# Weaving the first four scan steps of a channel tile between the last four of the tile before

## The chip, the cores and the metric

The kernel runs on one core of a Trainium2 chip, in one launch, all in fp32. The metric is the device time of that core in microseconds (us). Three runs of the kernel before took 17002.24, 17006.93 and 17012.62 us; the median, 17006.93 us, is the time before.

## What is computed

Two layers follow each other on a batch of eight images of 192 channels and 64 x 64 pixels. The change concerns the first, whose core is a gated scan in four directions over 384 channels:

```python
def gate_scan(X, L, Gl, Gm, Gr, chunk):        # chunk = 8: 8 steps, 8 chunks side by side
    h0 = zeros(B, C, H, W // chunk)
    def step(h, inp):
        x, l, gl, gm, gr = inp
        hn = l * x + gl * shift_up(h) + gm * h + gr * shift_down(h)
        return hn, hn
...
x = dwconv3x3(conv1x1(x, W_in)) + b_dw
p = conv1x1(x, W_xd)                           # 16 channels
xs = the 4 directions of x: rows, columns, and both reversed
Gl, Gm, Gr = the three parts of conv1x1(p, W_w), each divided by |Gl| + |Gm| + |Gr| + 1e-7
out = gate_scan(xs, conv1x1(p, W_l), Gl, Gm, Gr, 8) * conv1x1(p, W_u) + xs * conv1x1(p, W_d)
y = sum over d of w_m[d] * out[d]
y = conv1x1(grn(layernorm(y)), W_out)
```

The first of the eight steps of a scan starts from a state of zero. So it is only `l * x`: the gates Gl, Gm and Gr, their norm and the neighbours drop out of it. The second layer, two Mamba blocks on the 64 x 64 tokens of each image, is not touched.

## The kernel before, in words

The first layer is tile_ss2d_kernel. It goes through the images one by one. While the projections and the depthwise convolution of image b run, the normalisation and the output projection of image b-1 are woven in; then `scan` (line 347) runs alone.

A scan has 96 steps: 3 channel tiles c of 128 channels, 8 steps j, 4 directions d, in this order of nesting. A step works on 128 partitions x 512 elements (8 chunks x 64). The state of direction d is one tile of `states` (line 104), with a column of zeros on either side, and is used again by the next channel tile.

What a step does is cut into short methods of the class Step, one or a few instructions each. The order of the work is written out by hand: the kernel is built in manual_schedule, so that each engine gets its instructions in the order in which the Python code issues them. The loop at line 361 lays four steps over each other: s0 computes its neighbour products and norm, s1 its sum, s2 its state and output products, s3 its output sums, and `ahead` starts its gates. The parts that matter here, by engine:

- TensorE: `gates` and `up` (line 237) multiply 16 projected channels with the gate weights. A step has six gates, a step with j=0 only three (l, then d and u). `total` (line 273) adds the neighbour products by two matmuls with the identity. `add` (line 329) adds the two output products of the four directions in PSUM, again with the identity; for d=2 (JOINED) the second one is left out, and GpSimd has joined it to that of d=3 (line 315).
- VectorE: `neighbour` (L263, three products), `norm` (L278, two additions), `newton` (L294, L295), `mix` (L299) and `output` (L319). A j=0 step has only the last.
- ScalarE: absolute values (L247, L250), logarithm and exponential for the reciprocal (L283, L288), the copies of two gates from PSUM to SBUF, `decay` (L254, lam) and `direct` (L310, dx), and `store` (L339), which copies the sum of four directions out.
- GpSimd: `entry` (L257, l times x), `pair` (L267), `state` (L303) and `bypass` (L313, and L315 for d=3).

[...]gl, gm, q and yp one each, gr and c two each. The gates l, d and u of every step take turns in the two buffers of "c"; a buffer is free again when its gate has been copied by ScalarE (l, d) or multiplied by VectorE (u). In SBUF "dx" and "hu" have two buffers each. The pools reuse whichever buffer has become free, and the instruction that writes into it waits for the last one that used it.

## Time and profile before

| | us |
|---|---|
| median of three runs | 17006.93 |
| the profiled execution | 16998.62 |
| its span, first to last instruction | 16996.8 |
| first layer (until the last output copy at 5974.1) | about 5990 |
| TensorE busy, whole span | 15880.5 (93%) |
| VectorE busy | 15268.1 (90%) |
| GpSimd busy | 15164.6 (89%) |
| ScalarE busy | 11938.6 (70%) |

In the profile PE is TensorE, DVE VectorE, ACT ScalarE and POOL GpSimd. A line of a timeline gives the start of an instruction or of a run of equal ones in us from the start of the span, its duration, engine, line, operation, output and inputs, and in brackets how long the engine had been idle before it and what ended that. An fp32 matmul has two records here, so x4 after a line stands for two matmuls. A line of the table of stages gives the stretch, its length, the busy time and number of instructions of PE, PE's weight loads, DVE, ACT and POOL, then the clock that TensorE was granted (1.00 is full), the share of the DMA engines and GB/s.

The eight scans take some 520 to 530 us each from their first store to their last. Their boundaries between channel tiles, two in each scan, are 16 in all. In the middle of a tile all four compute engines run almost without pause: in the stretch from 264 to 287 us PE is busy for 23.0 of 23 us, DVE for 22.6, POOL for 22.4 and ACT for 15.4. In the stretch from 304 to 327 us, at a boundary, it is 22.3, 13.3, 20.8 and 9.3.

### The profile page before, as it was taken

The page shows a single profiled execution, that of the slowest core. Times are in us where ns is not written, and L with a number is a line of the kernel's source. Part 1 is how long each engine was busy: PE and PEld are TensorE (multiplying, and loading weights), DVE is VectorE, ACT ScalarE, POOL GpSimd, SP SyncE. Part 2 cuts the span into 40 slices and gives each one's busy share as a digit, 9 for nine tenths or more (in the row PEclk, how much of TensorE's full clock was granted, in tenths as well). Part 3 has the DMA queues.
Part 4 walks back from the last instruction along what each step waited for, and adds up shares of the span by engine and source line. Part 5 has one row for each costly group of instructions (what it writes and reads, how often), then busy time and mean ns, then how long its engine had stood idle before and what let it go on. Part 6 is the DMA issues. An engine that isn't in the chain of part 4 may idle for free.

```text
span 16996.8 us, 151143 instructions
## 1 busy us (share of the span) xinstructions
PE 15880.5 (93%) x42192; PEld 6479.2 (38%) x42192; DVE 15268.1 (90%) x14474; ACT 11938.6 (70%) x25451; POOL 15164.6 (89%) x9955
## 2 busy tenths in 40 slices
PE   9999999999999989999999999999999999999998
PEld 2333333333333334444444444444444444444443
DVE  8888888888887779999999999999999999999999
ACT  5656666666666667777777777777777777777777
POOL 7787978778787779999999999999999999999999
PEclk8999999999999999999999999999999999999999
DMA  1001010010100022222222222222222222222222
GB/s 30 24 7 30 1 30 9 22 30 1 30 1 26 3 95 105 105 105 105 104 106 104 106 104 106 104 106 104 106 104 106 104 106 104 106 104 103 106 102 87
DMA packets 695389, 1247.33 MB, mean 73 GB/s; under 512 B 311768, under 2 KB 378672, under 8 KB 694544
## 3 DMA queue, kind: packets, MB, share of 16 engines
q1 hardware_dynamic: 694144, 1237.37, 19.9%
q8 instruction: 335, 5.49, 0.1%
q14 instruction: 510, 4.18, 0.1%
q10 hardware_dynamic: 400, 0.29, 0.0%
HBM read 1178.77 MB, written 58.72 MB: 73 GB/s over the span
## 4 chain that ended last, share of the span: by engine, by line
DVE 26%; ACT 9%; POOL 9%; issue 8%; DMA 8%; PE 5%; SPq 0%; DVEq 0%; POOLq 0%; ACTq 0%
DVE da L848 18%; DMA c_sb<-bc 7%; POOL hs L834 6%; ACT da L840 3%; DVE hs L855 3%; DVE hs L848 3%; PE yp L860 2%; PE dbl_ps L721 1%; POOL hs L855 1%; DVE z L786 1%; DMA b_sb<-bc 1%; ACT xc L713 1%; ACT L713 1%; POOL e L756 1%; ACT xt L650 1%
## 5 line engine op out<-in xcount | busy, mean ns | idle before, releaser
L834 POOL TENSOR_TENSOR hs<-dtx,b_sb 128x1022 f32<-128x1022 f32 x3072 | 7140.1, 2351 | 62.1 <-DMA b_sb<-bc 29.8
L848 DVE TENSOR_TENSOR_SCAN da<-da,hs 128x1024 f32<-128x1024 f32 x2560 | 5852.5, 2286 | 497.0 <-ACT hs L843 462.8
L860 PE MATMUL yp<-hs,ident 128*128 128x512 f32 x12288 | 5764.5, 603 | 47.9 <-POOL hs L855 25.4
L840 ACT ACTIVATE da<-dt,a 128x512 f32<-128x512 f32 x6144 | 4246.7, 691 | 435.9 <-DVE hs L848 257.5
L860 PEld LDWEIGHTS yp<-hs,ident 128*128 128x128 f32 x12288 | 2316.7, 193 | 3058.9 <-issue 2700.9
L855 DVE TENSOR_TENSOR hs<-da,c_sb 128x1024 f32<-128x1024 f32 x2560 | 3129.3, 1222 | 88.4
L237 PE MATMUL g<-xp,w_gate_sb 16*128 16x512 f32 x8640 | 1816.2, 658 | 60.4 <-ACT dx L310 51.6
L851 ACT COPY state<-da 128x2 f32<-128x2 f32 x2560 | 399.4, 156 | 1981.8 <-DVE hs L855 1972.8
L700 PE MATMUL pc<-xr,conv_diag 128*128 128x512 f32 x3072 | 1572.3, 642 | 170.4 <-ACT dt L746 151.9
L678 PE MATMUL pi<-xT,in_w 96*128 96x512 f32 x3072 | 1447.2, 597 | 79.3 <-ACT y L816 36.5
L263 DVE TENSOR_TENSOR q<-g,h 128x512 f32<-128x512 f32 x2016 | 1351.4, 684 | 115.5 <-PE g L237 70.0
L273 PE MATMUL q<-q,ident 128*128 128x512 f32 x2688 | 1333.5, 619 | 0.0
L283 ACT ACTIVATE rc<-g,eps 128x512 f32<-128x512 f32 x672 | 462.0, 687 | 1116.7 <-DVE g L278 1116.7
L313 POOL TENSOR_TENSOR dx<-dx,xc 128x512 f32<-128x512 f32 x768 | 1079.5, 1406 | 156.6 <-ACT dx L310 133.6
L848 DVE TENSOR_TENSOR_SCAN hs<-da,hs 128x1024 f32<-128x1024 f32 x512 | 1167.5, 2280 | 57.2 <-POOL hs L834 57.2
L855 POOL TENSOR_TENSOR hs<-hs,c_sb 128x1024 f32<-128x1024 f32 x512 | 1204.9, 2353 | 1.2 <-ACT state L851 1.2
L267 POOL TENSOR_TENSOR q<-q,q 128x512 f32<-128x512 f32 x672 | 852.7, 1269 | 196.5 <-DVE q L263 190.9
L237 PEld LDWEIGHTS g<-xp,w_gate_sb 16*128 16x128 f32 x8640 | 495.0, 188 | 1304.9 <-DVE q L263 394.3
L700 PEld LDWEIGHTS pc<-xr,conv_diag 128*128 128x128 f32 x3072 | 584.8, 198 | 1029.0 <-issue 660.8
L257 POOL TENSOR_TENSOR lam<-lam,xc 128x512 f32<-128x512 f32 x672 | 942.0, 1402 | 33.3 <-ACT lam L254 33.3
L278 DVE TENSOR_TENSOR g<-g,ab 128x512 f32<-128x512 f32 x1344 | 933.0, 694 | 22.8
L196 DVE SCALAR_TENSOR_TENSOR xc<-pi,dw_sb,xc 128x504 f32<-128x504 f32 (+3 forms) x1152 | 839.5, 736 | 98.4 <-POOL xc L162 63.8
(140 smaller groups left out, 22975.2 us busy)
## 6 DMA issues: line engine op xcount, KB each, us to landing
b_sb<-bc SPq DMA_DIRECT2D x1024, 512.0 KB, 9.0
c_sb<-bc SPq DMA_DIRECT2D x1024, 512.0 KB, 8.9
xin<-in_x_dram SPq DMA_DIRECT2D x192, 384.0 KB, 3.6
mid<-ot SPq DMA_DIRECT2D x128, 192.0 KB, 2.1
xt<-mid SPq DMA_DIRECT2D x64, 384.0 KB, 10.0
out_dram<-y SPq DMA_DIRECT2D x64, 384.0 KB, 2.6
bc<-dbl SPq DMA_DIRECT2D x128, 64.0 KB, 1.6
b<-bc SPq DMA_DIRECT2D x128, 8.0 KB, 7.3
```

The costliest lines, as they stand in the source:

```text
L237: nc.tensor.matmul(dst, self.wg[r, at, self.d, :], flat(self.xp[r, self.j]), start=True, stop=True)
L257: nc.gpsimd.tensor_mul(self.lam if self.j else self.hc, self.lam, direction(self.xc, self.d, self.j))
L263: nc.vector.tensor_mul(self.q[i], rows(self.g[i]), self.h[:, :, i : i + HW])
L273: nc.tensor.matmul(self.sum, ident, flat(term), start=(i == 0), stop=(i == 1))
L313: nc.gpsimd.tensor_mul(self.dx, self.dx, direction(self.xc, self.d, self.j))
L678: nc.tensor.matmul(pi, self.m.in_w[:, i, c * P : (c + 1) * P], self.tokens.xT[:, i, :], start=(i == 0), stop=(i == 1))
L700: nc.tensor.matmul(pc, self.m.conv_w[:, c, t, :], self.xr[c][:, t : t + T], start=(t == 0), stop=(t == 3))
L834: nc.gpsimd.tensor_mul(self.hs[:, :, 1:], dtx, self.p.b_sb[self.g][:, :, 1:])
L840: nc.scalar.activation(self.da[:, n, :], self.p.dt[self.c], AF.Exp, scale=self.p.m.a[:, self.c, at : at + 1])
L848: nc.vector.tensor_tensor_scan(h, da, hs, 0.0, ALU.mult, ALU.add)
L855: engine.tensor_mul(self.hs, self.h, self.p.c_sb[self.g])
L860: nc.tensor.matmul(self.p.yp[self.c], ident, self.hs[:, n, :], start=False, stop=stop)
```

## The change

The steps of a scan are put in another order. At each of the two boundaries the four j=0 steps of the next channel tile, which stood behind the four j=7 steps of the tile that ends, are set between them: j=7 d=0, j=0 d=0, j=7 d=1, j=0 d=1 and so on. The loop that overlaps steps is as before. Since two channel tiles are now under way at once, there are eight states, four for even and four for odd tiles. The output sum of a tile needs the one bank "yp" until its last step, so the woven steps don't use it: their products are added by VectorE, straight into the output tile y in SBUF (seven additions for the four directions), and neither the store nor the joining of d=2 and d=3 is done for them. The j=0 steps of the first channel tile stay as they were.

```diff
-    for d in range(ND):
+    for d in range(2 * ND):
         states.append(const.tile([P, CHUNK, HW + 2], F32, name=f"h{d}"))
         nc.gpsimd.memset(states[d], 0.0)
...
-            self.h = states[d]
+            self.h = states[c % 2 * ND + d]
+
+            self.beside = c > 0 and j == 0
...
-            if self.d == JOINED + 1:
+            if self.d == JOINED + 1 and not self.beside:
                 nc.gpsimd.tensor_add(self.dx, self.dx, self.before.dx)
...
+            term = (self.hu, self.dx)[i]
+            if self.beside:
+                if self.d or i:
+                    nc.vector.tensor_add(self.y, flat(term if self.d else self.hu), self.y if self.d else flat(term))
+                return
...
-            if self.d == ND - 1:
+            if self.d == ND - 1 and not self.beside:
                 nc.scalar.copy(self.y, self.yp)
...
-        ys, steps = [], [Nothing()] * 4
+        ys = [big.tile([P, CHUNK, CHUNK * HW], F32, tag="big", name=f"y_{b}_{c}") for c in range(NC)]
+        done = []
         for c in range(NC):
...
+            tile = []
             for j in range(CHUNK):
...
+                for d in range(ND):
+                    tile.append(Step(f"{b}_{c}_{j}_{d}", xc[c], xp, ys[c][:, j, :], c, d, j))
+                    tile[-1].before = tile[-2] if d else None
+
+            for last, step in zip(done[-ND:], tile[:ND]):
+                done.insert(done.index(last) + 1, step)
+            done += tile[ND if c else 0 :]
+        steps = [Nothing()] * 4 + done
```

More of the change, by code (lines that the diff above doesn't have):

```diff
@@ L218, with __init__ @@
     class Step:
-        def __init__(self, tag, xc, xp, wg, d, j):
-            self.tag, self.xc, self.xp, self.wg, self.d, self.j = tag, xc, xp, wg, d, j
+        def __init__(self, tag, xc, xp, y, c, d, j):
+            self.tag, self.xc, self.xp, self.y, self.d, self.j = tag, xc, xp, y, d, j
+            self.wg = w_gate_sb[:, :, :, c * P : (c + 1) * P]
             self.q, self.ab = {}, {}
-            self.h = states[d]
+            self.h = states[c % 2 * ND + d]
+            self.beside = c > 0 and j == 0
             self.hc = self.h[:, :, 1 : HW + 1]
@@ L331, in add @@
                     ident,
-                    flat((self.hu, self.dx)[i]),
+                    flat(term),
                     start=(self.d == 0 and i == 0),
@@ L347, in scan @@
     def scan(b, xc, xp):
-        ys, steps = [], [Nothing()] * 4
+        ys = [big.tile([P, CHUNK, CHUNK * HW], F32, tag="big", name=f"y_{b}_{c}") for c in range(NC)]
+        done = []
         for c in range(NC):
-            wg = w_gate_sb[:, :, :, c * P : (c + 1) * P]
-            ys.append(big.tile([P, CHUNK, CHUNK * HW], F32, tag="big", name=f"y_{b}_{c}"))
+            tile = []
             for j in range(CHUNK):
-                steps += [Step(f"{b}_{c}_{j}_{d}", xc[c], xp, wg, d, j) for d in range(ND)]
-                for step in steps[-ND:]:
-                    step.y = ys[c][:, j, :]
-        for before, step in zip(steps[4:], steps[5:]):
-            step.before = before
+                for d in range(ND):
[5 more added lines that the diff above has]
+        steps = [Nothing()] * 4 + done
         steps += [Nothing()] * 4
```

## The prediction

> **What bounds the kernel now.** The page's busy table comes first, to rank the engines:

> ```profile
> PE 15880.5 (93%) x42192; PEld 6479.2 (38%) x42192; DVE 15268.1 (90%) x14474; ACT 11938.6 (70%) x25451; POOL 15164.6 (89%) x9955
> ```

> Three engines lie within four points, so the stage decides. Second, TensorE's timeline inside a channel tile. One step's cycle:

> ```profile
> 269.94 1.98 PE L273 MATMUL q<-q,ident 128*128 128x512 f32 x4
> 271.86 1.14 PE L237 MATMUL g<-xp,w_gate_sb 16*128 16x512 f32 x8
> 272.93 1.13 PE L329 MATMUL yp<-hu,ident 128*128 128x512 f32 x2
> 273.89 1.02 PE L329 MATMUL yp<-dx,ident 128*128 128x512 f32 x2
> 274.84 1.13 PE L237 MATMUL g<-xp,w_gate_sb 16*128 16x512 f32 x4
> ```

> Start to start: neighbour sum 1.92 us, four gates 1.07 (or a lone one, 1.05), two output sums 0.96 each, two gates 1.06. No line has an idle bracket: TensorE is the bound. A step is 5.95 us, 5.10 where d=2 leaves out one output sum, so four take 22.97 us. Third, ScalarE's timeline at a tile's end, which clocks the groups of four by their store:

> ```profile
> 309.64 0.61 ACT L339 COPY y<-yp 128x512 f32<-128x512 f32 x1
> ...
> 334.08 0.58 ACT L339 COPY y<-yp 128x512 f32<-128x512 f32 x1 [2.96 <-PE yp L329]
> ...
> 358.72 0.60 ACT L339 COPY y<-yp 128x512 f32<-128x512 f32 x1
> ...
> 381.75 0.60 ACT L339 COPY y<-yp 128x512 f32<-128x512 f32 x1
> ```

> From the store of j=6 to that of the next tile's j=1 pass 72.1 us here; over the 16 tile boundaries 67.5 to 73.4, mean 71.8. One plain group off, 48.8 us remain for j=7 and the next j=0 together, 25.8 more than j=7 alone. Why do four steps with a third of the work cost that? TensorE's timeline in the gentlest boundary, then the stages' clock in the first:

> ```profile
> 1982.08 1.12 PE L237 MATMUL g<-xp,w_gate_sb 16*128 16x512 f32 x2 [0.67 <-ACT dx L310]
> 1983.13 1.13 PE L329 MATMUL yp<-hu,ident 128*128 128x512 f32 x2
> 1984.19 1.13 PE L237 MATMUL g<-xp,w_gate_sb 16*128 16x512 f32 x4
> 1986.06 2.07 PE L237 MATMUL g<-xp,w_gate_sb 16*128 16x512 f32 x2 [0.75 <-ACT dx L310]
> ```

> ```profile
> 315.00:320.00 5.00, 5.00 (x13) 1.75 (x12) 2.29 (x4) 1.17 (x2) 4.64 (x5) 1.00 0.00 0
> ...
> 325.00:330.00 5.00, 4.26 (x7) 1.00 (x6) 0.69 (x1) 0.58 (x1) 3.16 (x3) 0.50 0.00 0
> ```

> The brackets show a chain: with two PSUM buffers for "c", the next gate waits until ScalarE has copied the bypass gate (0.7 us). A j=0 step is 1.05 + 0.96 or 1.92 + 1.06 + 0.7 us. And the same gate then takes 2.07 instead of 1.12: the clock (third column from the end) is halved. Asked in slices of 0.2 us, the clock in the first boundary is at half for 10.2, 3.4 and 3.5 us, 17 in all; in the gentlest, where the excess is 21.5 us, once for 6.8.

> [...]before both drops TensorE idles only 0.7 us of 3.4. Weighting the matmuls by the rows they feed (an identity sum 128 of 128, a gate 16) sorts this trace: the windows from 1982.4 (0.41) and 320.0 fall, those from 1979.0 (0.48) and 1996.1 (0.45) hold[...]. That weighting is my reading. [...]

> **The change, part by part.** F0..F3 are the j=7 steps, Z0..Z3 the next tile's j=0 steps, now ordered F0 Z0 F1 Z1 F2 Z2 F3 Z3. The built program's order confirms it; the steps issue no DMA, so SP's queue is as before.

> *Removed at each boundary:* 7 output sums (TensorE, 7 x 0.96 = 6.7 us), one store (ScalarE, 0.6), one joining add (GpSimd, 1.23). *Added:* 7 VectorE additions, 7 x 0.60 = 4.2 us. Four memsets of 0.54 us at the start lie beside the first loads: nothing; uncovered, 2.2 us. *Moved:* per Z step two ScalarE copies, three gates, two GpSimd products (2.73 us the pair), one VectorE product.

> Loads per F+Z pair: TensorE 5.74 + 2.11 = 7.85; GpSimd 5.49 + 2.73 = 8.22; VectorE 5.66 + 0.60 + 1.05 = 7.31. By load alone four pairs need 33 us against 48.8, and the gain would be 16 x 16 = 250 us. I don't believe it, because the pair has a longer chain. Around TensorE's queue: neighbour sum of F 1.92, four gates of the next F 1.07, two output sums of the earlier F 1.92, its two gates 1.06; copy of its bypass gate 0.7 (ScalarE); lone gate of Z 1.05; copy of that 0.7, because the third use of "c" needs its bank; last gate of the earlier Z 1.05; only then the next neighbour sum, queued behind. Sum 9.5 us. What hid the copies before, the neighbour and output sums, Z no longer has: its output sums are the part that moved. VectorE stays inside: from the gates' start 4.9 us to the end of the two norm additions (as between 335.83, the gates, and 339.31 + 1.42), one addition, hu at 6.1, in time for the Z gates at 6.5.

> ```profile
> 337.11 0.69 DVE L263 TENSOR_TENSOR q<-g,h 128x512 f32<-128x512 f32 x1 [1.19 <-PE g L237]
> 338.10 1.29 DVE L263 TENSOR_TENSOR q<-g,h 128x512 f32<-128x512 f32 x2 [0.30 <-ACT ab L250]
> 339.31 1.42 DVE L278 TENSOR_TENSOR g<-g,ab 128x512 f32<-128x512 f32 x2
> ```

> Laid out at full clock from F0's first product: F0's neighbour sum ends at 7.6, as in the steady rows. F1's ends at 17.6 (10.0: this pair still carries output sums of an earlier full step), F2's at 27.2, F3's at 36.7. Then a new wait. "dx" has two buffers; F2's is held until F3 joins it, so F3's copy waits for the one of Z2, which VectorE frees with its addition. Behind F3's copy stand, on ScalarE, the logarithm of the next step and, on TensorE, the next four gates, which need the copied bank. Layout: gates 36.7, VectorE's products and norm to 41.5, addition, hu, addition to 43.4, copy 44.1, gates to 45.3, copy, gate to 47.0, neighbour sum to 48.9. In steady running that sum ends at 7.6: four pairs cost 41.4 us.

> *Half clock.* The present boundaries: the gentlest has 21.5 excess with 6.8 us at half clock, of which 6.1 worked, so 3.1 lost and 18.4 left; the mean 25.8 loses 7.4. After: between the output sums' end and the next neighbour sum lie 4.5 us per pair with gates alone, weight under 0.2[...]. Walking four phases through the chain: the clock falls once per such pair and the sum's end moves by 1.7, 3.1, 3.8 and 1.7, mean 2.6. This holds for F2 and F3: 5.2. For F1, with output sums between, two phases in three and 2.3: 1.5. The wait after F3 (8.3 us from 38.7 to 47.0) surely drops it: gates 1.07, gate 1.05, sum 1.92 doubled, 4.1. Sum 10.8.

> [...]Unseen, so bounded: nothing if an addition only pushes GpSimd back (it has 1.3 us of room per 9.5); a whole product of 1.2 to 1.5 us ahead of hu for F3 and the step after, and again ahead of F3's copy: 4. [...]I take 1.5.

> Together 41.4 + 10.8 + 1.5 = 53.7 against 48.8: 4.9 us longer, times 16 = 78 us. The profiled execution took 16,998.6 (span 16,996.8), 8 below the median 17,006.9; 17,077 in its terms, 17,085 for the median. The second layer and the stages between scans are untouched.

> **Rivals.** *The clock holds* (other side): if Z's gates beside denser steps keep TensorE at full speed, 41.4 + 1.5 = 42.9, 5.9 less, 94 us: 16,913. It decides wherever less than 5.9 us per boundary is lost to half clock. For it: fewer bare j=0 steps in a row, and a threshold I inferred. Against: 4.5 us of gates alone. *The clock costs what it does now:* 41.4 + 7.4 + 1.5 = 50.3, 24 us more: 17,031. [...]4 us plus as much lost clock behind it, 57 or more: 17,150 to 17,200. That the change doesn't do what it says is excluded by the order.

> **Numbers.** The measurement tells about 0.2% (34 us) from no change. Forecast, slower, 0.45; clock holds, faster, 0.25; clock as now, same, 0.18; port, slower, 0.12. So faster 0.25, same 0.18, slower 0.57. Range 16,915 to 17,195; the slower cases alone 17,041 to 17,195.

> **What would show it.** Right: stores of j=6 to j=1 near 77 us; no output sums between the gates of Z and the next neighbour sum, brackets of 0.7 there; F3's copy idle on a VectorE addition; half-clock spells in the F2 and F3 pairs. Wrong: clock 1.00 through the boundary; the pair near 8.2 with GpSimd full (the chain misread); additions far above 0.7 us or GpSimd products stretched (port).

## The result, and the profile after

| | before | after |
|---|---|---|
| median of 5 runs, us | 17006.93 | 17079.14 |
| lowest to highest, us | 17002.24 to 17012.62 | 17070.02 to 17084.80 |
| ratio after/before, 95% interval | | 1.0043, 1.0032 to 1.0055 |
| span of the profiled execution, us | 16996.8 | 17067.9 |
| mean granted TensorE clock | 0.962 | 0.956 |

The change makes the kernel slower by 72 us, 0.4%. The forecast was 17,085.

The busy table of the page after:

```profile
PE 15913.8 (93%) x41968; PEld 6479.9 (38%) x41968; DVE 15377.4 (90%) x14586; ACT 11942.2 (70%) x25435; POOL 15168.9 (89%) x9943
```

TensorE has 224 records fewer (112 output sums) and is yet busy for 33 us more; VectorE has its 112 additions. A TensorE that does less work in more time is the first sign of its clock, whose mean fell from 0.962 to 0.956.

Next, ScalarE's timeline at the first tile boundary, the stores that clock the groups of four:

```profile
306.74 0.59 ACT L347 COPY y<-yp 128x512 f32<-128x512 f32 x1 [0.36 <-PE yp L337]
354.09 0.59 ACT L347 COPY y<-yp 128x512 f32<-128x512 f32 x1 [1.50 <-PE yp L337]
384.18 0.60 ACT L347 COPY y<-yp 128x512 f32<-128x512 f32 x1
```

They are the stores of j=6, j=7 and the next tile's j=1; the one between is gone. They lie 77.4 us apart here, 75.2 to 81.6 over the 16 boundaries, mean 78.5. In the changed kernel the store of j=6 itself comes earlier, so this pair holds a little of what was before it. A wider stretch is fairer, from the store of j=5 to that of the next tile's j=3. Its mean went from 140.7 to 146.1 us, 5.4 per boundary, 87 in all. The other parts of a scan, measured between the same stores, are the same to 0.1 us in both (114.9 before the first stretch, 45.9 between the two, 83.2 behind the second). The remaining -16 of the span's difference lie outside these stretches, -10 of it behind the last scan, for the most part in the second layer, which wasn't changed.

TensorE's timeline in that boundary (idle brackets as before):

```profile
299.69 1.14 PE L240 MATMUL g<-xp,w_gate_sb 16*128 16x512 f32 x8
300.76 1.13 PE L337 MATMUL yp<-hu,ident 128*128 128x512 f32 x2
301.81 1.13 PE L240 MATMUL g<-xp,w_gate_sb 16*128 16x512 f32 x4
303.67 1.12 PE L240 MATMUL g<-xp,w_gate_sb 16*128 16x512 f32 x2 [0.72 <-ACT dx L313]
...
312.59 1.13 PE L240 MATMUL g<-xp,w_gate_sb 16*128 16x512 f32 x4
314.44 3.92 PE L240 MATMUL g<-xp,w_gate_sb 16*128 16x512 f32 x6 [0.72 <-ACT dx L313]
318.29 3.78 PE L276 MATMUL q<-q,ident 128*128 128x512 f32 x4
322.01 1.64 PE L240 MATMUL g<-xp,w_gate_sb 16*128 16x512 f32 x8
...
335.94 1.13 PE L240 MATMUL g<-xp,w_gate_sb 16*128 16x512 f32 x4
340.01 4.73 PE L240 MATMUL g<-xp,w_gate_sb 16*128 16x512 f32 x12 [2.95 <-DVE hu L322]
344.67 3.78 PE L276 MATMUL q<-q,ident 128*128 128x512 f32 x4
...
358.53 1.40 PE L240 MATMUL g<-xp,w_gate_sb 16*128 16x512 f32 x4 [0.43 <-DVE hu L322]
```

The reader is to see three things. The brackets of 0.72 before the lone gates of Z1 and Z2 (303.67, 314.44) are the chain through "c". At 318.29 a neighbour sum (two matmuls) takes 3.78 us instead of 1.98: the granted clock is 0.50 there. And ahead of 340.01 TensorE stands for 2.95 us. The bracket names VectorE's hu, which freed one of the two buffers of "c". But ScalarE's timeline shows what was late, since its copy would have freed the other one some 2 us earlier. This is an estimate: F3's gates end at 337.07, and a gate behind such a copy waits 0.7 us.

```profile
340.67 0.59 ACT L313 COPY dx<-g 128x512 f32<-128x512 f32 x1 [3.58 <-DVE y L330]
341.15 0.69 ACT L286 ACTIVATE rc<-g,eps 128x512 f32<-128x512 f32 x1
```

This is F3's copy, waiting for its buffer until VectorE has added Z2's product (L330), with the logarithm behind it. The same 3.58 us stand there in all 16 boundaries.

Last, the table of stages at 3.4 us a row (the clock is the third column from the end):

```profile
333.40:336.80 3.40, 3.40 (x16) 0.91 (x14) 2.04 (x4) 1.78 (x4) 2.05 (x2) 1.00 0.00 0
336.80:340.20 3.40, 0.45 (x6) 0.19 (x8) 3.37 (x7) 0.29 (x1) 1.96 (x2) 0.99 0.00 0
340.20:343.60 3.40, 3.40 (x11) 1.37 (x12) 1.50 (x3) 2.74 (x6) 2.19 (x2) 0.50 0.00 0
343.60:347.00 3.40, 3.40 (x6) 1.18 (x4) 3.33 (x6) 1.53 (x4) 2.65 (x3) 0.50 0.00 0
```

In the second row TensorE works 0.45 us of 3.4, while VectorE is full (3.37) with products, norm, addition, hu and addition; the row after runs at half clock, and that lasts to 353.8. In slices of 1 us the stretch contains 30.1 us at half clock per boundary, against 16.6 before.

### One account for all kernels

For each kernel the stretch splits into three parts: TensorE's waits (those of gates and neighbour sums on hu, dx, lam and rc in the first layer, divided by 16), what is lost to half clock (an estimate: half of the time at half clock, since a neighbour sum then took 3.78 us instead of 1.98 and a lone gate 2.07 instead of 1.12), and the rest, TensorE's work at full speed. All in us per boundary; the ratio is to the kernel before on the same chip.

| kernel | ratio (95%) | stretch | waits | lost to half clock | rest |
|---|---|---|---|---|---|
| before | 1 | 140.7 | 3.2 | 8.3 | 129.2 |
| after | 1.0043 (1.0032 to 1.0055) | 146.1 | 6.5 | 15.0 | 124.6 |
| e1 own dx buffer | 1.0012 (1.0006 to 1.0019) | 142.7 | 5.6 | 13.0 | 124.1 |
| e2 after, fillers | 0.9992 (0.9985 to 0.9999) | 139.3 | 2.2 | 2.5 | 134.6 |
| e3 e1 and fillers | 0.9974 (0.9964 to 0.9983) | 138.7 | 2.0 | 4.5 | 132.2 |
| e4 e1, one addition | 1.0015 (1.0008 to 1.0021) | 143.4 | 3.5 | 14.5 | 125.4 |
| e5 before, fillers | 0.9966 (0.9953 to 0.9978) | 136.1 | 0.4 | 1.9 | 133.8 |
| e6 after, old order | 1.0012 (1.0006 to 1.0019) | 141.9 | 5.5 | 13.9 | 122.5 |
| e7 after, later sums | 1.0093 (1.0078 to 1.0109) | 149.6 | 1.8 | 20.7 | 127.1 |
| e8 before, thin fillers | 0.9986 (0.9980 to 0.9993) | 139.8 | 0.4 | 7.3 | 132.1 |
| e9 e7 and fillers | 1.0021 (1.0012 to 1.0029) | 142.5 | 1.6 | 4.6 | 136.3 |
| e10 e6 and fillers | 1.0004 (0.9996 to 1.0012) | 141.2 | 2.3 | 6.1 | 132.8 |
| e11 before, wide gates | 0.9925 (0.9912 to 0.9939) | 133.8 | 3.2 | 1.8 | 128.8 |
| e12 e1 and wide gates | 0.9980 (0.9972 to 0.9988) | 140.1 | 5.8 | 10.5 | 123.8 |

After against before: 4.6 us less work for TensorE, 3.3 more of waiting, 6.7 more lost to half clock, 5.4 in sum. That the rest is much the same (124.6, 124.1, 125.4, 123.8) in the four woven kernels without fillers or later sums supports the account. In every kernel 0.4 of the waits lies at the ends of the scans and not in the stretch; it drops out of the differences.

### The profile page after: what moved, and what is told of

The parts are those of the page before. It is cut to its first block, busy times and chain, and to the rows that moved or that the text cites. A ratio compares the mean times of both kernels' runs of the same rounds, so it can differ in the third digit from the quotient of the medians.

```text
span 17067.9 us, 150795 instructions
## 1 busy us (share of the span) xinstructions
PE 15913.8 (93%) x41968; PEld 6479.9 (38%) x41968; DVE 15377.4 (90%) x14586; ACT 11942.2 (70%) x25435; POOL 15168.9 (89%) x9943
## 4 chain that ended last, share of the span: by engine, by line
DVE 27%; ACT 9%; POOL 9%; issue 8%; DMA 7%; PE 4%; SPq 0%; DVEq 0%; POOLq 0%; ACTq 0%
DVE da L859 19%; DMA c_sb<-bc 6%; POOL hs L845 6%; DVE hs L866 4%; ACT da L851 3%; DVE hs L859 3%; POOL hs L866 1%; PE dbl_ps L732 1%; PE yp L871 1%; DVE z L797 1%; DMA b_sb<-bc 1%; ACT xc L724 1%; ACT L724 1%; POOL e L767 1%; POOL lg L769 1%
## 5 line engine op out<-in xcount | busy, mean ns | idle before, releaser
L240 PE MATMUL g<-xp,w_gate_sb 16*128 16x512 f32 x8640 | 1895.3, 676 | 107.2 <-DVE hu L322 52.9
L276 PE MATMUL q<-q,ident 128*128 128x512 f32 x2688 | 1443.2, 662 | 5.7 <-DVE rc L302 5.7
L306 POOL TENSOR_TENSOR h<-lam,rc 128x512 f32<-128x512 f32 x672 | 856.8, 1275 | 167.4 <-DVE rc L302 166.7
L260 POOL TENSOR_TENSOR lam<-lam,xc 128x512 f32<-128x512 f32 x672 | 940.7, 1400 | 30.1 <-ACT lam L257 29.6
```

The source lines that it names most:

```text
L240: nc.tensor.matmul(dst, self.wg[r, at, self.d, :], flat(self.xp[r, self.j]), start=True, stop=True)
L260: nc.gpsimd.tensor_mul(self.lam if self.j else self.hc, self.lam, direction(self.xc, self.d, self.j))
L276: nc.tensor.matmul(self.sum, ident, flat(term), start=(i == 0), stop=(i == 1))
```

## The experiments

The theory behind the prediction: the woven order gives TensorE spells of gates alone, so its clock is halved for longer, and the buffer of dx adds a wait. Rivals: VectorE's additions are what costs, by their own time or by what they and GpSimd's products lose to each other (in the changed kernel a product of 1.27 us took 2.01 and an addition of 0.68 took 1.28); or the longer chain costs by itself, and the clock only follows. The kernel before, run again beside each series of experiments, took 16,999.67 to 17,006.93 us as the median, so a difference of some 7 us between runs of different series says nothing.

### e1: a dx buffer of its own for d=2

```diff
-            self.dx = self.work("dx")
+            self.dx = self.work("dj", 1) if self.d == JOINED and not self.beside else self.work("dx")
```

> The changed kernel, with a buffer of its own for the bypass product of d=2 (of every step that is not woven), so that the copy for d=3 no longer waits until VectorE has added that of the woven step. My theory: TensorE's idle stretch of 3 us before the gates after the last pair goes, and with it part of the half-clock spell of 13.6 us that follows: 4 to 6 us per boundary, 16,985 to 17,015 us. Rival, the additions themselves[...] make the change slow and the buffer is a detail: under 1 us per boundary, 17,060 to 17,080.

Measured: 17,022.82, 56 below the change, 22 above before. Both theories had the sign, and the time is 8 above the upper end of the theory's. No copy into dx waits for an addition any more. This is worth 3.4 us per boundary (146.1 to 142.7), of which 0.9 is TensorE's waiting and 2.0 half clock, but it is not all that the change costs.

### e2: identity matmuls in the weave

```diff
+            fill(0 if not (getattr(s1, "beside", False) is True) else 4 if s1.d == ND - 1 else 1)
             ahead.gates()
...
+            fill(1 if getattr(s1, "beside", False) is True else 0)
```

`fill(n)` issues n matmuls of the identity with 128x512 of xc into the bank q; nobody reads the result. It stands ahead of and behind the gates of the iterations whose s1 is woven, four times ahead of the last.

> The changed kernel with useless identity matmuls into the free bank q, where TensorE waits between the output sums and the next neighbour sum: one before and one after the woven step's gate, four before the gates that wait longest. Nothing reads them. My theory (weight per window sets the clock): the clock stays at full speed through the boundary; some 27 us at half clock per boundary, about 10 of them lost, are saved, at a cost of 0.3 us per filler that is longer than the wait it sits in: 8 us per boundary less, about 16,950 us, faster than before too. Rival (the clock falls for another reason, or the chain of copies, not the clock, makes the boundary long): the half-clock spells stay and ten added matmuls of 0.96 us cost 2 to 9 us per boundary, 17,110 to 17,220 us.

Measured: 16,986.54, 93 below the change, although TensorE has 11 more matmuls of 0.96 us per boundary. The theory said 16,950: the sign is right, the size too hopeful. Half clock fell from 30.1 to 4.9 us per boundary. TensorE's timeline now shows a pair of 10.2 us with hardly a gap, so the fillers' own time eats part of the gain. The buffer's wait is still there (ScalarE idle for 3.58 us ahead of 339.20), now beside four fillers on TensorE.

### e3: both

Edit of e1, and one filler on either side of the gates.

> Both: the buffer of its own for d=2 and one filler before and one after the gates wherever the step ahead of the neighbour sum is a woven one. My theory: the layout at full clock without the buffer wait, 38 to 40 us in place of 48.8 before and 53.7 after: 16,840 to 16,880 us. Rival[...]: no better than the better of the two alone, 16,950 or more.

Measured: 16,954.12. That is 74 above the theory's range. It lies at the edge of the rival's range of time, but the rival is wrong too in what it said, since this is 32 better than the better of the two alone. The two edits of 56 and 93 give 125 together. What stays: TensorE itself is full in the pairs (10.2 us), and behind the weave lies a wait that no edit touched:

```profile
352.71 1.89 PE L240 MATMUL g<-xp,w_gate_sb 16*128 16x512 f32 x4 [1.16 <-DVE hu L322]
354.64 3.78 PE L276 MATMUL q<-q,ident 128*128 128x512 f32 x4
```

It is the iteration in which Z3 would add its outputs on TensorE. It has nothing to add, TensorE runs ahead of VectorE, and the clock falls once more.

### e4: e1 without six of the seven additions

```diff
-                if self.d or i:
+                if self.d == 0 and i:
```

It leaves out the outputs of d=1, 2 and 3 at j=0 of the second and third tile.

> As the kernel with the buffer of its own for d=2, but of the seven additions of a boundary only the first is left: the outputs of directions 1 to 3 are left out at j=0 of the second and third channel tile. [...]My theory: 1 to 2 us per boundary, 15 to 35 us less than the kernel with the additions. Rival[...]: 4 to 8 us per boundary, 65 us or more less.

Measured: 17,023.25, the same as e1. The additions, with what they and GpSimd's products lose to each other, cost nothing that shows in the time, and neither expectation held (15 to 35 below e1, or 65 and more). But TensorE waits less without them (3.5 for 5.6 us), and the half clock takes most of that back (14.5 for 13.0). What the additions would cost at full clock isn't shown.

### e5: the filler in the kernel before

```diff
+            fill(1 if bare(s1) else 0)
             ahead.gates()
```

`bare` is true for the j=0 steps of the second and third tile.

> The kernel before, with one identity matmul of 128x512 into a bank of the pool q (its result is not read) ahead of the gates in each iteration whose s1 is a step of j=0 of the second or third channel tile: it stands where the missing neighbour sum would stand. If the half clock is what a boundary loses, before as after, then before has it too: some 16.6 us at half clock per boundary, at about 0.45 us each 7.4 us, less some 1 to 1.5 us that the four matmuls (0.94 us each) cost where nothing hides them. Theory: half clock in the stretch below 6 us per boundary, time 16,890 to 16,930, and the change made on top of fillers (the earlier run with fillers, 16,986) is then slower than this by 50 or more. Rival, the clock is only a sign and the waits for VectorE and GpSimd set the boundary: 17,000 to 17,030, with the half clock gone or not.

Measured: 16,940.41, at 3.8 us of half clock. The theory held, with a time 10 us above its range and e2 46 us slower than this where 50 or more was expected. The rival, that the clock is only a sign, is out: it had 17,000 to 17,030. The boundaries of this one kernel also price the half clock: 13 of 16 have none and take 134.3 us, the three others have 20.5 and take 144.1. So 9.8 us are lost to 20.5 at half clock.

With fillers in both, the woven order gains nothing: 16,954 (e3, with the buffer mended) against 16,940, two ratios whose intervals overlap. The feeding isn't equal, though: e3 carries eight fillers per boundary where e5 has four, and it still has 9.0 us at half clock.

### e6: the old order, with the additions kept

```diff
-            for last, step in zip(done[-ND:], tile[:ND]):
-                done.insert(done.index(last) + 1, step)
-            done += tile[ND if c else 0 :]
+            done += tile
```

> The changed kernel with its order undone: the four steps of j=0 follow the last four of the tile before, as in the kernel before; eight states and VectorE's additions of the outputs stay. So TensorE has neither neighbour sum nor output sum in four iterations that follow each other, while the chain (gates, copies, product, state) stays the one of the kernel before. Theory, the time is set by the chain and by the clock, and TensorE is fed least here: four iterations without sums are some 4 x 1.92 us less work for TensorE, which the chain doesn't let through, the half clock as long as before or longer (16 to 25 us per boundary): 17,000 to 17,080. Rival 1, the weaving itself is what makes the change slower and the additions are harmless or a gain: below 17,000. Rival 2, VectorE's additions are what costs: as slow as the changed kernel, 17,080 or more.

Measured: 17,022.51, within the theory's range. So moving the output sums to VectorE costs 18 us by itself, with no weave. It takes TensorE's work at the boundary from 129.2 to 122.5 us and gives 5.6 back to half clock and 2.3 to waits. The weave without its buffer wait (e1) has the same ratio; the wait is the other 56.

### e7: the sums spread over the woven iterations

Three buffers for dx, the two output sums of an F step one iteration later, on either side of the woven step's lone gate, and Z's lam copied ahead of the logarithm.

```diff
-            self.dx = self.work("dx")
+            self.dx = self.work("dx", 3)
...
+            if behind and woven:
+                s4.add(0)
             ahead.gates()
...
+            if behind:
+                s4.add(1)
```

> The changed kernel with three edits at the boundary: three buffers for dx (and for the squares that share them); the output sums of the last four steps of a tile are issued one iteration later, so that each iteration of the weave, the woven step's too, has work for TensorE of nearly the same amount; and the woven step's lam is copied ahead of the logarithm on ScalarE. Theory, the boundary is set by the chain through the two gates and by the clock that falls for want of matmuls in the woven iterations: with the work spread the half clock falls from 30 us per boundary to below 10, worth some 9 us, and the buffer's wait is gone, worth some 4 us: 13 x 16 = 200 below the changed kernel, 16,860 to 16,920. Rival, what holds the boundary is VectorE and GpSimd by their own work, and the clock follows: 16,960 to 17,030, little better than the run with the one buffer alone (17,023).

Measured: 17,151.21. Both expectations were wrong: it is the slowest of all. And it is the most telling, since TensorE hardly waits in it (1.8 us per boundary) and loses 20.7. The table of stages:

```profile
311.40:314.80 3.40, 3.40 (x15) 1.05 (x13) 2.03 (x4) 1.76 (x4) 2.03 (x2) 1.00 0.00 0
314.80:318.20 3.40, 3.40 (x4) 0.92 (x4) 3.25 (x6) 0.81 (x2) 3.21 (x3) 0.50 0.00 0
```

and what ran in the first of these rows (after 0.43 us of a neighbour sum) and at the start of the second, the last two lines at half clock already:

```profile
311.83 2.97 PE L241 MATMUL g<-xp,w_gate_sb 16*128 16x512 f32 x12
314.73 2.07 PE L338 MATMUL yp<-hu,ident 128*128 128x512 f32 x2
316.73 2.07 PE L241 MATMUL g<-xp,w_gate_sb 16*128 16x512 f32 x2
```

TensorE was busy without a break (3.40 of 3.40), and the clock fell: the row was gates, each of which feeds 16 of 128 rows (they overlap: four took 1.14 us together in the changed kernel, at 299.69, and a lone one 1.12, at 303.67). From 314.8 to 342.1 it then stayed at half, again without a gap. I had spread the waiting; what counts is something else.

### e8 and e11: nearly the same time, other rows

e8 is e5 with fillers of 16 rows:

```diff
-                    bank("q", f"fill_{b}"), ident, xc[0][:, :8, :].rearrange("p h w -> p (h w)"), start=True, stop=True
+                    bank("q", f"fill_{b}"), w_gate_sb[0:RANK, 0, 0, 0:P], flat(xp[0:RANK, 0]), start=True, stop=True
```

> The kernel before with fillers, but each filler is a product with 16 rows instead of 128: a weight of 16x128 and 16x512 of the gates' input, into the same bank at the same place. It keeps TensorE busy for the same time. Theory, the clock of the next 3.41 us follows the share of a window in which products with 128 rows run[...]: the fillers of 16 rows count for nothing, half clock 14 us or more per boundary, 17,000 to 17,060. Rival, any busy TensorE holds the clock and the gap of 0.7 us is what lets it fall: as with the fillers of 128 rows, half clock below 6 us, 16,930 to 16,950.

Measured: 16,977.55, with 14.5 us of half clock where e5 has 3.8, and the same waits (0.4). On the clock the theory held; the time lies 22 below its range, as the fillers took the place of gaps and cost little. Such a filler takes 0.83 to 0.95 us where the identity took 1.05, but in both kernels TensorE has no gap left in the stretch. So a busy TensorE alone didn't keep the clock here: with fillers of 128 rows 3.8 us at half clock were left, with those of 16 rows 14.5.

e11 is the kernel before with no filler. Only the l gate of the j=0 steps is fed with all 128 rows, by a weight that is zero in 112 of them:

```diff
...
+            if self.j == 0 and self.c and kind in WIDE:
+                w = w_wide[:, WIDE.index(kind), self.d, (self.c - 1) * P : self.c * P]
+                nc.tensor.matmul(dst, w, flat(self.xp[:, self.j]), start=True, stop=True)
+                return dst
```

> The kernel before, with no filler; only the l gate of the j=0 steps of the second and third channel tile is fed with all 128 rows of the gates' input (its weight has zeros in the 112 others, so its result is the same). Such a gate stands alone and takes about 1 us with 16 rows as an identity matmul does with 128, so TensorE is busy for the same time. Theory, the rows that a window feeds set the next window's clock: each j=0 iteration then has 1.92 or 2.88 us of 128-row work, most windows lie above 0.4, the half clock falls from 16.6 us per boundary to below 6, the stretch from 140.7 to 132 to 136 (the waits of 0.7 us for ScalarE's copies stay): time 16,890 to 16,940. Rival, the clock follows the gaps or the busy time, not the rows: half clock 14 us or more, time 16,985 to 17,015.

Measured: 16,875.98, ratio 0.9925 (0.9912 to 0.9939), 14 better than the theory's range and faster than both kernels. TensorE's timeline in the first boundary:

```profile
319.40 1.13 PE L249 MATMUL g<-xp,w_gate_sb 16*128 16x512 f32 x4
321.20 1.12 PE L247 MATMUL g<-xp,w_wide 128*128 128x512 f32 x2 [0.67 <-ACT dx L322]
322.16 1.02 PE L341 MATMUL yp<-hu,ident 128*128 128x512 f32 x2
323.12 1.13 PE L249 MATMUL g<-xp,w_gate_sb 16*128 16x512 f32 x4
324.99 1.13 PE L247 MATMUL g<-xp,w_wide 128*128 128x512 f32 x2 [0.74 <-ACT dx L322]
```

The gaps of 0.67 and 0.74 are those of the kernel before, whose clock fell behind the first of them, so that its gate after the second took 2.07 us instead of 1.13:

```profile
322.53 1.14 PE L237 MATMUL g<-xp,w_gate_sb 16*128 16x512 f32 x2 [0.67 <-ACT dx L310]
323.60 2.08 PE L329 MATMUL yp<-hu,ident 128*128 128x512 f32 x2
325.60 2.08 PE L237 MATMUL g<-xp,w_gate_sb 16*128 16x512 f32 x4
328.43 2.07 PE L237 MATMUL g<-xp,w_gate_sb 16*128 16x512 f32 x2 [0.74 <-ACT dx L310]
```

TensorE's waits for dx, in the list of waits of the first layer, are the same in both, 51.6 us before and 29.0 + 22.6 here:

```profile
PE g L237 <- ACT dx L310: 51.6, 72, 0.7
```

```profile
PE g L249 <- ACT dx L322: 29.0, 40, 0.7
PE g L247 <- ACT dx L322: 22.6, 32, 0.7
```

No instruction and no wait went from TensorE's queue. What went is the half clock, 16.6 to 3.6 us per boundary, and with it 6.9 us of the stretch, 110 us in all. By the account 6.5 of these are the clock; the other 0.4 is TensorE's own work, where for one an output sum starts 0.86 us behind a wide gate (316.74 to 317.60) instead of 1.05 behind a thin one (317.77 to 318.82 in the kernel before). This is the cleanest pair of the study. It doesn't separate the rows of the weight from those of the moving data: both have 128.

### e9, e10 and e12: is the weave worth anything once the clock is fed?

e9 is e7 with one filler ahead of the woven step's gates and one ahead of the sum where that step is s3; e10 is e6 with the same.

> The changed kernel with the later output sums, three dx buffers and the earlier lam copy (17,151), and in addition one identity matmul with 128 rows between the gates of each woven iteration and one ahead of the sum two iterations later. Theory, that kernel lost its time to the clock alone (41 us at half clock per boundary, worth 18 to 19, of 149.6): with the clock held its stretch is 131 to 135, time 16,860 to 16,930, 220 to 290 below the run without fillers. Rival, the waits inside the woven pairs set it: less than 100 below, 17,050 or more.

> The changed kernel in the old order (17,022) with one identity matmul with 128 rows ahead of the gates in each iteration whose s1 is a step of j=0, and one ahead of the sum where s3 is. At full clock this shows what VectorE's additions alone are worth, without the weave: the stretch of that kernel, 141.9 with 27.7 us at half clock, would be some 129.5 at full clock, and the fillers cost between 0 and 4. Theory: half clock below 6 us, 129.5 to 134, time 16,830 to 16,920. Rival, the additions stand in VectorE's queue ahead of products that the chain needs, and hold the boundary back once TensorE is at full clock: as the kernel before with fillers or slower, 16,940 or more.

e9 measured 17,037.72: 113 below e7, between the theory's 220 to 290 and the rival's less than 100. Half clock fell to 9.2 us, and the fillers filled TensorE instead, a pair taking 10.8 us without a gap. e10 measured 17,009.34, where 16,830 to 16,920 was expected: it still has 12.2 us at half clock, and the rest grew by 10.3 us, of which the eight fillers explain 7.7. Both times I had taken the fillers for nearly free; they aren't where the queue is already full. For e10 the rival's time came about, but its reason, VectorE's queue, isn't shown: TensorE waits less than in e6 (2.3 for 5.5).

e12 is e1 with the wide l gate, three buffers instead of four for the input images making room.

> The changed kernel with the own dx buffer for the step d=2 (17,023 without more) and with the l gate of the woven steps fed with 128 rows, as in the last run of the kernel before (16,876). To make room for its weights the input images have three buffers instead of four, which may cost some 10 us between the scans. Question: is the weave worth anything once its gates are fed? By the accounting of that kernel (stretch 142.7, of which 5.3 wait and 13 are lost to half clock) 129.7 would be left at full clock, 2.3 less than the 132.0 of the kernel before in its undisturbed boundaries. Theory: the bare spell of a woven pair, two gates, a wait of 0.7, the l gate, two gates, has only 0.96 us of 128-row work in 3.9 us, a share of 0.28 in the worst window[...]: half clock 8 to 20 us per boundary, 16,900 to 16,990, not faster than 16,876. Rival: the clock holds and the output sums that TensorE no longer does come through as time: half clock below 4 us, 16,800 to 16,860.

Measured: 16,970.65, inside the theory's range, with 20.9 us at half clock, a little above it. One wide gate in a woven pair's bare spell didn't hold the clock, where in the old order 3.6 us at half clock were left with it. So 95 us lie between the two orders with the same feeding (ratios 0.9980 and 0.9925, intervals apart). The smaller number of input buffers isn't the reason: the time between the scans is 1,470 us in all, against 1,474 in the kernel before.

## Why the prediction was right, by its steps

- *TensorE bounds the inside of a tile:* right. The three parts of a scan off the boundaries didn't move.
- *The load count promises 250 us, and the chain takes it:* right. F1's neighbour sum ends 9.9 us after F0's (299.69 to 309.60, forecast 10.0). With their half clock, F2's followed after 12.4 (9.6 + 2.6) and F3's after 11.8 (9.5 + 2.6).
- *At full clock both layouts take the same:* nearly. Forecast 41.4 against 41.4 (48.8 less 7.4); by the account, rest and waits together are 131.1 against 132.4, a gain of 1.3.
- *F3's copy waits for the addition of Z2:* right, with 3.58 us idle at L313 and 56 us back in e1. The next sum came 14.6 us later where 16.3 was laid out.
- *Half clock:* it comes where the forecast put it and carries the result; its sizes were small. Forecast 10.8 lost against 7.4, 3.4 more; by the account 15.0 against 8.3, 6.7 more. Two places were missed. The half clock that the wait after F3 sets off was counted up to the next neighbour sum, but in the first boundary it lasts 13.7 us, to 353.8, so that from the first to the second sum of the next tile's j=1 steps pass 8.6 us instead of 5.95. And in the iteration with Z3 as s3 the clock falls again (360.6 to 364.0). The weighting by rows, the author's reading of four windows, sorts those of both kernels (last section).
- *VectorE's additions beside GpSimd's products, 1.5:* wrong as a cost. The trace of before doesn't show that the two hold each other up; the 1.5 was the author's estimate. In the changed kernel they do, but what an addition loses doesn't reach the end (e4), where the clock takes back what the waits give. The timelines of GpSimd and VectorE:

```profile
327.44 2.01 POOL L316 TENSOR_TENSOR dx<-dx,xc 128x512 f32<-128x512 f32 x1
```

```profile
327.39 0.68 DVE L330 TENSOR_TENSOR y<-hu,y 128x512 f32<-128x512 f32 x1
```

The addition that came first ran its 0.68 us, and GpSimd's product took 2.01 instead of the 1.27 of the one at 314.52; beside that one, where GpSimd was first, the addition at 315.07 took 1.28. Why they do so isn't shown.

So 0 + 3.4 + 1.5 = 4.9 was forecast and -1.3 + 6.7 + 0 = 5.4 measured per boundary. That the total was closer than its terms is luck: half clock too low by 3.3, set off by the additions (1.5 too high) and the layout (1.3).

Of the rivals, "the clock costs what it does now" fails by the 15.0 against 8.3, and the case that the forecast calls "port", in which the additions and GpSimd's products hold VectorE up by 4 us per boundary, by e4. "The clock holds" had a flaw that the runs show. It counted the weave's gain against a boundary that loses to half clock itself. Feed the clock there, and the old order takes 16,876; the weave then has nothing to take.

What stays open: TensorE's work fell by 4.6 us per boundary where 6.7 (seven output sums) were taken away; and e10's rest isn't accounted for in full.

## What to carry to other kernels

Moving work off an engine can make the rest slower: seven sums moved from TensorE to VectorE gave 18 us away in the old order, as 5.6 us per boundary went back to half clock. Before an order is rebuilt to shorten a boundary, ask what part of that boundary is half clock: here it was 8.3 of 140.7 us, and feeding one lone gate with 128 rows took most of it back at no cost in TensorE's time. Count the instructions that a woven stage puts between two uses of a double buffer, since a wait of 3.6 us behind one "dx" was over two thirds of the loss.

## What the runs showed of the hardware that I had not expected

The prediction's weighting by rows sorts these pieces better. Each record of a matmul is given 0.43 us of the piece, 0.85 at half clock (two records of 0.43 are the 0.86 us of e11 above), times the share of the 128 rows that it feeds: 1 for an identity, 0.125 for a gate. At full clock, half clock followed on all 106 pieces with a weight up to 0.367 and on none of the 982 from 0.374 up. If the gates counted for nothing, 50 pieces would lie in a range (0.223 to 0.304) where it went both ways. At half clock, full clock followed on none of the 100 pieces below 0.733 and on all 85 above 0.804; on the 34 between it went both ways. The pieces from 1982.4, 1979.0 and 1996.1, for which the prediction has 0.41, 0.48 and 0.45, weigh 0.34, 0.43 and 0.39 by this count.

These are counts of two traces, in whose stretches all matmuls have 16 or 128 rows; what sets the clock isn't shown by them.

The matmul with 128 rows needn't do anything: with a weight that is zero in 112 of 128 rows (e11), 3.6 us at half clock were left per boundary, and 3.8 with an identity whose result nobody reads (e5), of 16.6 in the kernel before.
